# The adjacency test of a graph network moved from the loading to a second read beside layer 1, with the rows' transposes put between the chunks of the first product

## The chip, the cores and the metric

The kernel runs on one core of a Trainium2 chip. The metric is device time in microseconds (us) of one execution. Engines are named as in the profile: PE is TensorE, PEld its weight loads, DVE is VectorE, ACT is ScalarE, POOL is GpSimd, and SPq is the DMA queue issued from SyncE. A load has *landed* when its data is there; the *granted clock* is the share of full speed that the profile records for PE. The batches are worked on in four *pairs*, the nodes in four *blocks* of 512.

## The reference, cut to what matters

```python
# x: 8 x 2048 x 64, adj: 2048 x 2048 fp32; a row of adj has one value where it is not zero
h = relu(layernorm(x)); x = x + L0(h, adj)   # Chebyshev terms h, A h, 2 A(A h) - h, node-wise weights
h = relu(layernorm(x)); x = x + L1(h, adj)   # 3 steps: v = W2 relu(W1 [v, A v] + b1) + b2
h = relu(layernorm(x)); x = x + L2(h, adj)   # one A h, then small matrices
h = relu(layernorm(x)); x = x + L3(h, adj)   # attention with mask adj > 0.5: for this adj a mean over nodes
```

The kernel keeps the adjacency as a 0/1 pattern `BT` (the sign of `adj`, transposed) and the row values apart (`crow`). That holds only if all non-zero values of a row are equal and none exceeds 0.5. So it *tests* the adjacency; if the test fails a general path runs. The test must read every element of `adj` and know its row's maximum.

## The kernel before: the parts that matter

Loading (32 half-rows of 128 x 1024, three buffers) with the test beside it:

```python
def load_adj(nb):                                   # one of 4 node blocks
    for t in range(4):
        i = 4 * nb + t
        for hf in range(2):
            st = prop.tile([P, N // 2], F32, name="st", bufs=3)
            nc.sync.dma_start(st, adj[i*P:(i+1)*P, hf*(N//2):(hf+1)*(N//2)])
            for q in range(2):                      # 8 transposes on PE, sign on ACT
                pt = transposed(...)
                nc.scalar.activation(BT[:, nb, m0:m0+4, t*P:(t+1)*P], pt, AF.Sign)
            c = cols2[:, i, hf:hf + 1]
            nc.vector.tensor_reduce(c, st, axis=AX.X, op=ALU.max)
            nc.vector.scalar_tensor_tensor(         # the test
                junk, st, c, st, op0=ALU.not_equal, op1=ALU.logical_and,
                accum_out=bad2[:, i, hf:hf + 1])
    ...                                             # crow of this block
```

The product that all layers use, 32 matmuls (a high part H and a low part L of the features, 16 chunks), and layer 1, whose step feeds the next one:

```python
def product(hl, nb, name, out, crow, mid=None):
    for m in range(NCH):
        for i in range(2):
            nc.tensor.matmul(ps, hl[m // 4][i][:, m % 4, :], BT[:, nb, m, :], ...)
        if m == NCH // 2 and mid is not None:
            mid()
    nc.vector.tensor_tensor(out, ps, crow, op=ALU.mult)

for s in range(3):                                  # layer 1, one pair of batches
    for nb in range(NB):
        ph = ...                                    # one matmul
        e = product(hl, nb, ..., mid=mid if nb == 3 else None)
        nc.vector.tensor_tensor(e, ph, e, op=ALU.add)
        nc.scalar.activation(g, e, AF.Relu, bias=...)
        if nb in (1, 2): finish(nb - 1)             # bn on PE, then H and L of the next step
    ...
```

The order in the source is not the order on the engines: the scheduler of the framework places each instruction where its data and engine allow.

Of the kernel before, what the change touches and what calls it, by code (L numbers as in the profile page):

```python
# [40 lines left out]
def uniform_path(  # L41
# [53 lines left out]
    def bank(tag, name):  # L95
        return psum.tile([P, 512], F32, tag=tag, name=name)
# [12 lines left out]
    def part(nb):  # L109
        return slice(4 * nb, 4 * nb + 4)  # L110

    def load_x(layer, p, nb):
        acc = block("acc", f"acc_{layer}_{p}_{nb}", 2)
        fill_x(acc, layer, p, nb)
        return acc

    def fill_x(acc, layer, p, nb):
        if layer == 0:
            for bb in range(2):
                nc.sync.dma_start(  # L120
                    acc[:, :, bb * C:(bb + 1) * C],
                    x[2 * p + bb].rearrange("(j p) c -> p j c", p=P)[:, part(nb), :],
                )
        else:
            nc.sync.dma_start(acc, xs[p][:, part(nb), :])
# [41 lines left out]
        nc.vector.tensor_tensor(Lq, src, Hq.bitcast(F32), op=ALU.subtract)  # L167
        return Hq, Lq

    def product(hl, nb, name, out, crow, mid=None):  # L170

        ps = bank("mm", f"bv_{name}")
        for m in range(NCH):
            for i in range(2):
                nc.tensor.matmul(  # L175
                    ps, hl[m // 4][i][:, m % 4, :], BT[:, nb, m, :],
                    start=(m == 0 and i == 0), stop=(m == NCH - 1 and i == 1),
                )
            if m == NCH // 2 and mid is not None:
                mid()  # L180
        nc.vector.tensor_tensor(out, ps, crow, op=ALU.mult)  # L181
        return out

# [17 lines left out]
    def term(k, name):  # L201
        return l0f.tile([P, 512], F32, tag=f"t{k}", name=name, bufs=(4, 4, 2)[k])

    def norm_0(p, nb):
        return norm_relu(load_x(0, p, nb), f"0_{p}_{nb}")


    cols2 = consts.tile([P, NCH, 2], F32, name="cols2")
    bad2 = consts.tile([P, NCH, 2], F32, name="bad2")
    cols = consts.tile([P, NCH, 1], F32, name="cols")  # L210
    pro = ExitStack()
    prop = pro.enter_context(tc.tile_pool(name="prop", bufs=1))

    def load_adj(nb):
        for t in range(4):
            i = 4 * nb + t
            for hf in range(2):
                st = prop.tile([P, N // 2], F32, name="st", bufs=3)
                nc.sync.dma_start(st, adj[i * P:(i + 1) * P, hf * (N // 2):(hf + 1) * (N // 2)])
                for q in range(2):  # L220
                    pt = transposed(
                        lambda m: st[:, (4 * q + m) * P:(4 * q + m + 1) * P], f"adj_{i}_{hf}_{q}"
                    )
                    m0 = 8 * hf + 4 * q
                    nc.scalar.activation(BT[:, nb, m0:m0 + 4, t * P:(t + 1) * P], pt, AF.Sign)  # L225
                c = cols2[:, i, hf:hf + 1]
                nc.vector.tensor_reduce(c, st, axis=AX.X, op=ALU.max)  # L227
                junk = prop.tile([P, N // 2], U8, name="junk")
                nc.vector.scalar_tensor_tensor(  # L229
                    junk, st, c, st, op0=ALU.not_equal, op1=ALU.logical_and,  # L230
                    accum_out=bad2[:, i, hf:hf + 1],
                )
        nc.vector.tensor_tensor(
            cols[:, part(nb), :], cols2[:, part(nb), 0:1], cols2[:, part(nb), 1:2], op=ALU.max
        )
        pg = transposed(lambda t: cols[:, 4 * nb + t, :].to_broadcast([P, P]), f"c_{nb}")
        crow = work.tile([P, 512], F32, tag="crow", name=f"crow_{nb}", bufs=2)
        nc.scalar.copy(crow, pg.rearrange("p t n -> p (t n)"))
        nc.gpsimd.dma_start(crowD[:, nb * 512:(nb + 1) * 512], crow[0:1, :])
        return crow  # L240

    def test():


        w = small.tile([P, NCH, 2], F32, name="w", bufs=1)
        nc.vector.tensor_tensor(w, cols2, cols.to_broadcast([P, NCH, 2]), op=ALU.not_equal)
        nc.vector.tensor_tensor(w, w, cols2, op=ALU.logical_and)
        nc.vector.tensor_tensor(bad2, bad2, w, op=ALU.add)
        for op, lim in ((ALU.is_gt, THRESHOLD), (ALU.is_lt, 0.0)):
            nc.vector.tensor_scalar(w, cols2, lim, None, op0=op)  # L250
            nc.vector.tensor_tensor(bad2, bad2, w, op=ALU.add)
        tot = small.tile([P, 1], F32, name="tot")
        nc.vector.tensor_reduce(tot, bad2.rearrange("p j h -> p (j h)"), axis=AX.X, op=ALU.add)
        pf = bank("tr", "pf")
        nc.tensor.matmul(pf[:1, :1], tot, ones[:, :1], start=True, stop=True)
        nc.vector.tensor_scalar(flag, pf[:1, :1], 0.0, None, op0=ALU.is_gt)




    def term1(p, hl, crow_of):
        t1T, hl1 = [], []

        def back(nb):
            pt = transposed(lambda t: t1T[nb][:, t * P:(t + 1) * P], f"t1_{p}_{nb}")
            hl1.append(halves(pt, f"t1_{p}_{nb}"))

        for nb in range(NB):
            crow = crow_of(nb)
            nm = f"0_{p}_{nb}a"  # L270
            t1T.append(product(
                hl, nb, nm, term(1, f"t1T_{nm}"), crow, mid=(lambda: back(2)) if nb == 3 else None
            ))
            if nb in (1, 2):
                back(nb - 1)
        back(3)
        return t1T, hl1

    t0T, hl = [], []
    for nb in range(NB):  # L280
        z = norm_0(0, nb)
        hl.append(halves(z, f"0_0_{nb}"))
        t0T.append(to_feat(z, term(0, f"t0T_0_{nb}"), f"0_0_{nb}"))
    t1T, hl1 = term1(0, hl, load_adj)
    test()
    pro.close()

    l0p = l0.enter_context(tc.tile_pool(name="l0p", bufs=1))
# [64 lines left out]
    for p in range(NP):  # L353
        if p > 0:
            t1T, hl1 = term1(p, hl, lambda nb: load_crow(nb, f"0_{p}_{nb}a"))
        hl_next, t0T_next = [], []

        def prepare(q):
            if p + 1 < NP:
                h = load_h(p + 1, q, f"0_{p + 1}_{q}")  # L360
                hl_next.append(halves(h, f"0_{p + 1}_{q}"))
                return h

        def prepare_feat(h, q):
            if p + 1 < NP:
                t0T_next.append(to_feat(h, term(0, f"t0T_{p + 1}_{q}"), f"0_{p + 1}_{q}"))

        for nb in range(NB):
            nm = f"0_{p}_{nb}b"
            crow = load_crow(nb, nm)  # L370
            pre = []
            t2T = product(
                hl1, nb, nm, term(2, f"t2T_{nm}"), crow,
                mid=(lambda: pre.append(prepare(2))) if nb == 3 else None,
            )
            if p + 1 < NP:

                for q in ((0, 1), (2, 3), (), ())[nb]:
                    nc.gpsimd.dma_start(hs[p + 1][:, part(q), :], norm_0(p + 1, q))
            if nb == 3:  # L380
                prepare_feat(pre[0], 2)
                h3 = prepare(3)
            node_weights(p, nb, (t0T[nb], t1T[nb], t2T))
            if nb in (1, 2):
                prepare_feat(prepare(nb - 1), nb - 1)
        if p + 1 < NP:
            prepare_feat(h3, 3)
        hl, t0T = hl_next, t0T_next
# [96 lines left out]
        hl.append(halves(h, nm))  # L485




    def layer1(n, p):  # L490
        hl, gT = ops[n]
        steps = 3
        for s in range(steps):
# [22 lines left out]
            for nb in range(NB):  # L516
                nm = f"1_{p}_{s}_{nb}"
                crow = load_crow(nb, nm)
                ph = bank("tr", f"ph_{nm}")
                nc.tensor.matmul(ph, w1v2 if s else w1vT, gT[nb], start=True, stop=True)  # L520
                e = product(hl, nb, nm, feat(f"e_{nm}"), crow, mid=mid if nb == 3 else None)
                nc.vector.tensor_tensor(e, ph, e, op=ALU.add)  # L522
                g = feat(f"g_{nm}")
                nc.scalar.activation(g, e, AF.Relu, bias=b1s if s else b1c)  # L524
                g_new.append(g)
                if nb in (1, 2):
                    finish(nb - 1)
                    if last:
                        prepare(n + 1, nb - 1)
            if last:  # L530
                finish(2)
                prepare(n + 1, 3)
# [5 lines left out]
    def layer2(n, p):  # L538
# [18 lines left out]
        for nb in range(NB):  # L557
            nm = f"2_{p}_{nb}"
            crow = load_crow(nb, nm)
            e = product(  # L560
                hl, nb, nm, feat(f"e_{nm}"), crow,
                mid=(lambda: prepare(n + 1, 2)) if nb == 3 else None,
            )
            finish(nb, e)
            if nb in (1, 2):
                prepare(n + 1, nb - 1)
# [17 lines left out]
        prepare(0, q)  # L584
    for n, (layer, p) in enumerate(items):
        (layer1, layer2)[layer - 1](n, p)


@with_exitstack
# [590 lines left out]
```

## Time and profile before

| | before |
|---|---|
| median of the runs at hand | 1509.42 us (1506.44 to 1510.51) |
| span of the profiled run | 1499.4 us (it took 1501.24, a quick one) |
| first product starts, last of the first four is scaled | 51.3 us, 127.7 us |
| first matmul of the node weights, `y` | 149.7 us |
| layer 1 of the first pair: first product scaled | 840.4 us |
| its three steps, product 0 to product 0 | 36.8, 36.8, 43.0 us |

The slices, the tile `st` and the queue's waits are in the prediction; they show a prologue of 128 us in which DVE is at 6 to 8 tenths, and the test among what holds the three buffers. To read the landmarks: the DVE row `t1T_3a<-bv_3a,crow` is the scaling of the last of the first four products, so its start is the end of the prologue. Before and after:

```profile
127.68 0.69 DVE L181 TENSOR_TENSOR t1T_3a<-bv_3a,crow 128x512 f32<-128x512 f32 x1 [1.67 <-PE bv_3a L175]
```

```profile
103.45 0.69 DVE L181 TENSOR_TENSOR t1T_3a<-bv_3a,crow 128x512 f32<-128x512 f32 x1 [1.89 <-PE bv_3a L175]
```

### The profile page before, as it was taken

What the parts mean: (1) busy time and instruction counts of PE and PEld (TensorE: products, weight loads), DVE (VectorE), ACT (ScalarE), POOL (GpSimd) and SP (SyncE); (2) the same over time, 40 slices, a digit from 0 to 9 for tenths busy, and PEclk for the clock granted to TensorE, in tenths of its full rate; (3) what the DMA queues carried; (4) which work ended last, traced back from release to release, by engine and by line L of the source; (5) the groups of instructions that cost most, each with busy time, mean ns of one, the idle gap of its engine ahead of it and who ended that gap; (6) DMA issues with size and microseconds to landing.
All of it is one profiled execution on the core that took longest, in us unless ns stands there. A gap on an engine that the chain in (4) does not pass through costs nothing.

```text
span 1499.4 us, 15921 instructions
## 1 busy us (share of the span) xinstructions
PE 1312.4 (88%) x6000; PEld 904.8 (60%) x6000; DVE 867.3 (58%) x1879; ACT 188.4 (13%) x317; POOL 242.8 (16%) x234
## 2 busy tenths in 40 slices
PE   2679978997989979899994999999999999898883
PEld 1567434563446534475442877777778777776762
DVE  6885777747777578736785223433523533655453
ACT  3341000000000000000000211211211211111000
POOL 2101111102102021110101001301300300424442
PEclk9999989998999989999997999999999999999897
DMA  3554112112112021110101002301301310323221
GB/s 106 192 189 110 46 53 64 43 46 70 46 36 69 20 70 46 40 53 21 46 29 45 34 28 59 103 29 57 112 28 43 119 32 32 135 70 113 92 85 30
DMA packets 83080, 99.04 MB, mean 66 GB/s; under 512 B 49332, under 2 KB 51380, under 8 KB 82996
## 3 DMA queue, kind: packets, MB, share of 16 engines
q1 hardware_dynamic: 75060, 73.30, 16.6%
q0 software_dynamic: 7936, 24.66, 4.6%
q8 instruction: 49, 0.80, 0.2%
q14 instruction: 35, 0.29, 0.1%
HBM read 73.28 MB, written 24.65 MB: 65 GB/s over the span
## 4 chain that ended last, share of the span: by engine, by line
PE 51%; DVE 24%; issue 12%; POOL 6%; DMA 4%; ACT 1%; SPq 1%; DVEq 0%; POOLq 0%; ACTq 0%
PE bv L175 24%; DVE acc L347 15%; POOL rstd L156 4%; PE y L340 4%; PE bn L466 3%; PE ph L520 3%; PE bv_0a L175 2%; PE bv_0b L175 2%; PE bv_3a L175 2%; PE bv_1a L175 2%; PE bv_2a L175 2%; DMA st<-in_adj_dram 2%; DVE z L157 2%; PE pS L552 1%; DVE var L153 1%
## 5 line engine op out<-in xcount | busy, mean ns | idle before, releaser
L175 PE MATMUL bv<-BT,H 128*128 128x512 f32 x1024 | 424.2, 414 | 0.0
L175 PE MATMUL bv<-BT,L 128*128 128x512 f32 x1024 | 408.3, 399 | 0.9 <-DVE L L167 0.9
L347 DVE SCALAR_TENSOR_TENSOR acc<-y,emb,acc 128x128 f32<-128x128 f32 x1024 | 355.3, 350 | 63.8 <-PE y L340 21.5
L175 PEld LDWEIGHTS bv<-BT,L 128*128 128x128 f32 x1024 | 194.2, 190 | 52.0 <-issue 9.3
L175 PEld LDWEIGHTS bv<-BT,H 128*128 128x128 f32 x1024 | 194.1, 190 | 49.9 <-issue 9.3
L340 PE MATMUL y<-wt,t0T 64*128 64x512 f32 x512 | 149.9, 653 | 67.8 <-DVE acc L347 64.6
L181 DVE TENSOR_TENSOR e<-bv,crow 128x512 f32<-128x512 f32 x64 | 44.2, 691 | 191.6 <-PE bv L175 191.3
L321 POOL DMA_DIRECT2D xs<-acc x32 | 17.8, 556 | 844.0 <-DVE acc L503 352.3
L156 POOL TENSOR_TENSOR rstd<-var,mhalf 128x8 f32<-128x8 f32 x64 | 108.1, 1689 | 220.7 <-DVE var L154 210.3
L340 PEld LDWEIGHTS y<-wt,t0T 64*128 64x128 f32 x512 | 45.3, 192 | 156.4 <-PE y L340 94.1
L151 ACT ACTIVATE sq<-z 128x512 f32<-128x512 f32 x64 | 40.5, 633 | 678.1 <-DVE z L147 668.2
L157 DVE SCALAR_TENSOR_TENSOR z<-z,rstd 128x512 f32<-128x512 f32 x64 | 53.8, 841 | 108.4 <-POOL rstd L156 108.4
L153 DVE TENSOR_REDUCE var<-sq 128x8 f32<-128x512 f32 x64 | 43.8, 685 | 31.2 <-ACT sq L151 31.1
L188 PE MATMUL pt_adj<-ident,st 128*128 128x128 f32 x256 | 40.5, 308 | 22.0 <-DMA st<-in_adj_dram 16.6
L188 PEld LDWEIGHTS pt_adj<-ident,st 128*128 128x128 f32 x256 | 31.9, 157 | 30.3 <-ACT BT L225 23.0
L552 PE MATMUL pS<-z,ones 128*128 128x128 f32 x128 | 22.8, 333 | 29.0 <-DVE z L157 29.0
L507 DVE TENSOR_TENSOR bn<-bn,r1e 128x512 f32<-128x512 f32 x32 | 22.2, 695 | 43.4 <-PE bn L466 43.4
L145 DVE TENSOR_REDUCE mean<-acc 128x8 f32<-128x512 f32 x64 | 43.3, 684 | 4.6 <-DMA acc<-in_x_dram 3.1
L524 ACT ACTIVATE g<-e,b1s 128x512 f32<-128x512 f32 x32 | 23.2, 726 | 178.6 <-DVE e L522 178.6
L147 DVE TENSOR_TENSOR z<-acc,mean 128x512 f32<-128x512 f32 x64 | 43.9, 694 | 1.7
L227 DVE TENSOR_REDUCE cols<-st 128x1 f32<-128x1024 f32 x32 | 38.9, 1218 | 9.8 <-DMA st<-in_adj_dram 9.7
L229 DVE SCALAR_TENSOR_TENSOR junk<-st,cols 128x1024 uint8<-128x1024 f32 x32 | 41.0, 1280 | 0.5
(185 smaller groups left out, 1777.2 us busy)
## 6 DMA issues: line engine op xcount, KB each, us to landing
st<-in_adj_dram SPq DMA_DIRECT2D x32, 512.0 KB, 4.1
crow<-crowD SPq DMA_DIRECT2D x64, 256.0 KB, 3.3
hs<-z POOLq DMA_DIRECT2D x44, 256.0 KB, 2.7
hb<-hs SPq DMA_DIRECT2D x44, 256.0 KB, 4.1
acc<-in_x_dram SPq DMA_DIRECT2D x64, 128.0 KB, 2.8
xs<-acc POOLq DMA_DIRECT2D x32, 256.0 KB, 2.7
acc<-xs SPq DMA_DIRECT2D x32, 256.0 KB, 4.0
out_dram<-acc POOLq DMA_DIRECT2D x32, 128.0 KB, 4.2
```

What stands on the lines that cost most here:

```text
L145: nc.vector.tensor_reduce(mean, groups(xt), axis=AX.X, op=ALU.add)
L147: nc.vector.tensor_tensor(g, groups(xt), mean[:, :, None].to_broadcast([P, 8, C]), op=ALU.subtract)
L153: nc.vector.tensor_reduce(var, groups(sq), axis=AX.X, op=ALU.add)
L156: nc.gpsimd.tensor_tensor(rstd, var, mhalf, op=ALU.pow)
L157: nc.vector.scalar_tensor_tensor(g, g, 0.0, rstd[:, :, None].to_broadcast([P, 8, C]), op0=ALU.max, op1=ALU.mult)
L175: nc.tensor.matmul(ps, hl[m // 4][i][:, m % 4, :], BT[:, nb, m, :], start=(m == 0 and i == 0), stop=(m == NCH - 1 and i == 1),)
L181: nc.vector.tensor_tensor(out, ps, crow, op=ALU.mult)
L188: nc.tensor.transpose(pt[:, t, :], src(t), ident)
L340: nc.tensor.matmul(y[:, bb, :], terms[k][hs_, ts], wt[hs_, k, dg * 512:(dg + 1) * 512], start=(k == 0), stop=(k == K - 1),)
L347: nc.vector.scalar_tensor_tensor(xj, y[:, :, d * C:(d + 1) * C], emb[:, 4 * nb + t, e:e + 1], xj, op0=ALU.mult, op1=ALU.add,)
L466: nc.tensor.matmul(ps[:, t, :], fT[:, t * P:(t + 1) * P], wmat, start=True, stop=True)
L520: nc.tensor.matmul(ph, w1v2 if s else w1vT, gT[nb], start=True, stop=True)
```

## The change

It means to take the test out of the loading, where DVE is full (6 to 8 tenths), and to do it where DVE idles (2 to 5 tenths in layers 1 and 2), on a second read of the adjacency beside layer 1. The loading is taken apart so that the transposes of the next block stand between the chunks of the current product.

```diff
-def load_adj(nb):
-    for t in range(4):
+def load_adj(nb, t):
...
-            nc.vector.scalar_tensor_tensor(junk, st, c, st, op0=ALU.not_equal, op1=ALU.logical_and, ...)
...
 t0T, hl = [], []
 for nb in range(NB):
+    load_adj(0, nb)
     z = norm_0(0, nb)                      # x of the first pair now loaded from the ACT queue
...
-t1T, hl1 = term1(0, hl, load_adj)
-test()
+def rows_between(nb):
+    return {4 * t + 1: (lambda t=t: load_adj(nb + 1, t)) for t in range(4)}   # empty for the last
+t1T, hl1 = term1(0, hl, make_crow, rows_between)
...
+def test(i):
+    for q in range(NB):
+        st = lastp.tile([P, 512], F32, name="st", bufs=2)
+        nc.sync.dma_start(st, adj[i*P:(i+1)*P, q*512:(q+1)*512])
+        nc.vector.scalar_tensor_tensor(junk, st, cols[:, i, :], st, ..., accum_out=bad[:, i, q:q+1])
...
 # layer 1, after each block
+if s < 2 and nb in (0, 2):
+    test(4 * p + 2 * s + nb // 2)          # meant: 16 row groups over four pairs
```

More of the change, by code (lines that the diff above doesn't have):

```diff
@@ L110, in part, with load_x, fill_x @@
         return slice(4 * nb, 4 * nb + 4)
-    def load_x(layer, p, nb):
+    def load_x(layer, p, nb, queue=nc.sync):
         acc = block("acc", f"acc_{layer}_{p}_{nb}", 2)
-        fill_x(acc, layer, p, nb)
+        fill_x(acc, layer, p, nb, queue)
         return acc
-    def fill_x(acc, layer, p, nb):
+    def fill_x(acc, layer, p, nb, queue=nc.sync):
         if layer == 0:
             for bb in range(2):
-                nc.sync.dma_start(
+                queue.dma_start(
                     acc[:, :, bb * C:(bb + 1) * C],
@@ L168, in halves, with product @@
         return Hq, Lq
-    def product(hl, nb, name, out, crow, mid=None):
+    def product(hl, nb, name, out, crow, fill={}):
         ps = bank("mm", f"bv_{name}")
@@ L178, in product @@
                 )
-            if m == NCH // 2 and mid is not None:
-                mid()
+            if m in fill:
+                fill[m]()
         nc.vector.tensor_tensor(out, ps, crow, op=ALU.mult)
@@ L204, in norm_0 @@
     def norm_0(p, nb):
-        return norm_relu(load_x(0, p, nb), f"0_{p}_{nb}")
+        return norm_relu(load_x(0, p, nb, nc.scalar if p == 0 else nc.sync), f"0_{p}_{nb}")
     cols2 = consts.tile([P, NCH, 2], F32, name="cols2")
-    bad2 = consts.tile([P, NCH, 2], F32, name="bad2")
     cols = consts.tile([P, NCH, 1], F32, name="cols")
@@ L212, in uniform_path, with make_crow @@
     prop = pro.enter_context(tc.tile_pool(name="prop", bufs=1))
-    def load_adj(nb):
-        for t in range(4):
-            i = 4 * nb + t
-            for hf in range(2):
-                st = prop.tile([P, N // 2], F32, name="st", bufs=3)
-                nc.sync.dma_start(st, adj[i * P:(i + 1) * P, hf * (N // 2):(hf + 1) * (N // 2)])
-                for q in range(2):
-                    pt = transposed(
-                        lambda m: st[:, (4 * q + m) * P:(4 * q + m + 1) * P], f"adj_{i}_{hf}_{q}"
-                    )
-                    m0 = 8 * hf + 4 * q
-                    nc.scalar.activation(BT[:, nb, m0:m0 + 4, t * P:(t + 1) * P], pt, AF.Sign)
-                c = cols2[:, i, hf:hf + 1]
-                nc.vector.tensor_reduce(c, st, axis=AX.X, op=ALU.max)
-                junk = prop.tile([P, N // 2], U8, name="junk")
-                nc.vector.scalar_tensor_tensor(
-                    junk, st, c, st, op0=ALU.not_equal, op1=ALU.logical_and,
-                    accum_out=bad2[:, i, hf:hf + 1],
-                )
+    def load_adj(nb, t):
+        i = 4 * nb + t
+        for hf in range(2):
+            st = prop.tile([P, N // 2], F32, name="st", bufs=3)
+            nc.sync.dma_start(st, adj[i * P:(i + 1) * P, hf * (N // 2):(hf + 1) * (N // 2)])
+            for q in range(2):
+                pt = transposed(
+                    lambda m: st[:, (4 * q + m) * P:(4 * q + m + 1) * P], f"adj_{i}_{hf}_{q}"
+                )
+                m0 = 8 * hf + 4 * q
+                nc.scalar.activation(BT[:, nb, m0:m0 + 4, t * P:(t + 1) * P], pt, AF.Sign)
+            nc.vector.tensor_reduce(cols2[:, i, hf:hf + 1], st, axis=AX.X, op=ALU.max)
+    def make_crow(nb):
         nc.vector.tensor_tensor(
@@ L240, in load_adj, with term1 @@
         return crow
-    def test():
-        w = small.tile([P, NCH, 2], F32, name="w", bufs=1)
-        nc.vector.tensor_tensor(w, cols2, cols.to_broadcast([P, NCH, 2]), op=ALU.not_equal)
-        nc.vector.tensor_tensor(w, w, cols2, op=ALU.logical_and)
-        nc.vector.tensor_tensor(bad2, bad2, w, op=ALU.add)
-        for op, lim in ((ALU.is_gt, THRESHOLD), (ALU.is_lt, 0.0)):
-            nc.vector.tensor_scalar(w, cols2, lim, None, op0=op)
-            nc.vector.tensor_tensor(bad2, bad2, w, op=ALU.add)
-        tot = small.tile([P, 1], F32, name="tot")
-        nc.vector.tensor_reduce(tot, bad2.rearrange("p j h -> p (j h)"), axis=AX.X, op=ALU.add)
-        pf = bank("tr", "pf")
-        nc.tensor.matmul(pf[:1, :1], tot, ones[:, :1], start=True, stop=True)
-        nc.vector.tensor_scalar(flag, pf[:1, :1], 0.0, None, op0=ALU.is_gt)
-    def term1(p, hl, crow_of):
+    def term1(p, hl, crow_of, between=lambda nb: {}):
         t1T, hl1 = [], []
@@ L271, in term1 @@
             t1T.append(product(
-                hl, nb, nm, term(1, f"t1T_{nm}"), crow, mid=(lambda: back(2)) if nb == 3 else None
+                hl, nb, nm, term(1, f"t1T_{nm}"), crow, fill={**({8: lambda: back(2)} if nb == 3 else {}), **between(nb)}
             ))
@@ L283, in uniform_path @@
         t0T.append(to_feat(z, term(0, f"t0T_0_{nb}"), f"0_0_{nb}"))
-    t1T, hl1 = term1(0, hl, load_adj)
-    test()
+    def rows_between(nb):
+        if nb + 1 == NB:
+            return {}
+        return {4 * t + 1: (lambda t=t: load_adj(nb + 1, t)) for t in range(4)}
+    t1T, hl1 = term1(0, hl, make_crow, rows_between)
     pro.close()
@@ L373, in uniform_path @@
                 hl1, nb, nm, term(2, f"t2T_{nm}"), crow,
-                mid=(lambda: pre.append(prepare(2))) if nb == 3 else None,
+                fill={8: lambda: pre.append(prepare(2))} if nb == 3 else {},
             )
@@ L485, in prepare, with test_end @@
         hl.append(halves(h, nm))
+    bad = lastp.tile([P, NCH, NB], F32, name="bad")
+    def test(i):
+        for q in range(NB):
+            st = lastp.tile([P, 512], F32, name="st", bufs=2)
+            nc.sync.dma_start(st, adj[i * P:(i + 1) * P, q * 512:(q + 1) * 512])
+            junk = lastp.tile([P, 512], U8, name="junk")
+            nc.vector.scalar_tensor_tensor(
+                junk, st, cols[:, i, :], st, op0=ALU.not_equal, op1=ALU.logical_and,
+                accum_out=bad[:, i, q:q + 1],
+            )
+    def test_end():
+        for op, lim in ((ALU.is_gt, THRESHOLD), (ALU.is_lt, 0.0)):
+            w = lastp.tile([P, NCH, 1], F32, name="w", bufs=2)
+            nc.vector.tensor_scalar(w, cols, lim, None, op0=op)
+            nc.vector.tensor_tensor(bad[:, :, 0:1], bad[:, :, 0:1], w, op=ALU.add)
+        tot = lastp.tile([P, 1], F32, name="tot")
+        nc.vector.tensor_reduce(tot, bad.rearrange("p i q -> p (i q)"), axis=AX.X, op=ALU.add)
+        pf = bank("tr", "pf")
+        nc.tensor.matmul(pf[:1, :1], tot, ones[:, :1], start=True, stop=True)
+        nc.vector.tensor_scalar(flag, pf[:1, :1], 0.0, None, op0=ALU.is_gt)
     def layer1(n, p):
@@ L520, in layer1 @@
                 nc.tensor.matmul(ph, w1v2 if s else w1vT, gT[nb], start=True, stop=True)
-                e = product(hl, nb, nm, feat(f"e_{nm}"), crow, mid=mid if nb == 3 else None)
+                e = product(hl, nb, nm, feat(f"e_{nm}"), crow, fill={8: mid} if nb == 3 else {})
                 nc.vector.tensor_tensor(e, ph, e, op=ALU.add)
@@ L561, in layer2 @@
                 hl, nb, nm, feat(f"e_{nm}"), crow,
-                mid=(lambda: prepare(n + 1, 2)) if nb == 3 else None,
+                fill={8: lambda: prepare(n + 1, 2)} if nb == 3 else {},
             )
@@ L586, in uniform_path @@
         (layer1, layer2)[layer - 1](n, p)
+        if n == NP - 1:
+            test_end()
 @with_exitstack
```

## The prediction

The 0.69 us of a 128x512 test is the mean of the 128x512 scaling in the trace before.

> **What bounds the kernel now.** I read four views: the slices of the page, to find stages in which TensorE (PE) is not full; the instructions on the adjacency tile `st` and the waits of the DMA queue, to see what holds the first stage; the timeline of PE there, for single intervals; and the timelines of layer 1, where the moved work goes.
>
> ```profile
> PE   2679978997989979899994999999999999898883
> DVE  6885777747777578736785223433523533655453
> DMA  3554112112112021110101002301301310323221
> ...
> L188 PE MATMUL pt_adj<-ident,st x256: 270/273/476, 31.5 to 121.6; 128*128 128x128 f32 x128
> L227 DVE TENSOR_REDUCE cols<-st x32: 1208/1220/1221, 8.2 to 120.5; 128x1 f32<-128x1024 f32 x32
> L229 DVE SCALAR_TENSOR_TENSOR junk<-st,cols x32: 1273/1280/1286, 9.9 to 121.7; 128x1024 uint8<-128x1024 f32 x32
> L229 DVE DVE_READ_ACCUMULATOR junk<-st,cols x32: 81/84/89, 11.1 to 122.9; 128x1 f32 x32
> ...
> DMA to landing us min/median/max: 3.1/4.1/5.3
> ...
> SPq L219 <- DVE junk L229: 56.9, 24, 3.9
> SPq L219 <- PE pt_adj L188: 25.0, 9, 11.4
> ```
>
> A slice is 37.5 us. In the first three PE is at 2, 6 and 7 tenths, VectorE (DVE) at 6, 8 and 8: this is the prologue, to about 128 us, in which 32 half-rows of the adjacency are loaded, transposed, reduced to their maximum and tested. The last two lines tell who holds the loads: with three `st` buffers a new load waits for the *test* 56.9 us in total and for the transposes 25.0 us, of which one wait is 11.4 us, because PE's first transpose of `st` is at 31.5 us, behind the normalisation of x. So the bound here is a ring of three buffers whose turn is landing (4.1 us) plus transposes plus maximum plus test, served by a DVE that is nearly full. PE's own work to 127.6 us is only about 63 us: four products of 32 x 0.2326 us (the spacing of their matmuls in the timeline) = 30, 256 transposes at 0.109 = 28, other transposes 5.
>
> From the second node block on the limits are others: layer 0 alternates PE and DVE (1024 multiply-adds of 350 ns), layers 1 and 2 have PE at 9 tenths and DVE at 2 to 5. Layer 1 of the first pair, on DVE and then PE:
>
> ```profile
> 867.99 0.69 DVE L181 TENSOR_TENSOR e<-bv,crow 128x512 f32<-128x512 f32 x1 [1.16 <-PE bv L175]
> 868.72 0.69 DVE L522 TENSOR_TENSOR e<-ph,e 128x512 f32<-128x512 f32 x1
> ...
> 867.79 1.02 PE L520 MATMUL ph<-g,w1v 128*128 128x512 f32 x2
> 870.26 1.12 PE L466 MATMUL bn<-w1e,g 128*128 128x128 f32 x8
> ```
>
> At the end of a step the last block's product is scaled at 867.99, added at 868.72, passed through ReLU to 870.16, and PE takes it at 870.26, seven matmuls into the next step. There is no slack: what delays this scaling delays PE.
>
> [...] the trace has 691 ns as the mean of the 128x512 scaling. I use it for the test at 512 columns, which the kernel before has only at 1024. [...] eight transposes took 1.94 us after 3.85 us of idle at 46.70[...].
>
> **The change, part by part.**
>
> *Taken from the prologue.* 32 tests: 32 x (1.20 us spacing + 0.08 read of the accumulator) = 41 us of DVE, and the closing test, 8 small operations of 0.2 us with one matmul, 1.6 us. DVE's 102 us of work before 130 us becomes about 60, so it stops being a limit, and the ring's turn loses the test.
>
> *Reordered.* The first adjacency rows are loaded before x, and the built program's PE order puts each later 128 rows' transposes between the chunks of the product before. First four row groups: a chain remains, since the same ACT queue copies transposes out and issues the second half of x. From the first load at about 1 us I followed normalisation (10 to 14 us for the first block, as now), x's third block issued near 19 us, its result near 31, the fourth near 36; the first product starts then, near 37 us, against 51.3 now. After that 24 half-rows remain. Per half-row PE needs 0.87 us of transposes and four chunks' share, 0.93, plus short waits for ACT: three products 22.3 + 24 x 0.87 + about 8 for waits and other transposes = 51 us. The loads need 24 x 512 KB = 12.6 MB; the best 10 us stretch now moved 244 GB/s, which is 51.6 us. Two limits this close disturb each other: I add 5 us. Product 2 ends near 93, product 3 (7.44 us and two transposes) near 101.5. It now ends at 127.6. Gain: 26 us.
>
> *Start of the node weights.* In the new order 12 instead of all 32 matmuls of the second b-product stand ahead of the first `y`. Now `y` starts at 149.66 although its inputs are ready at about 145.4. 20 x 0.2326 = 4.6 us; the 20 matmuls fall later where PE idles (4 us busy of 10 at 190). Gain: 4.6 us.
>
> *Added in layer 1.* 16.8 MB read again as 64 loads of 256 KB on the SP queue, and 64 tests of 128x512: 0.69 + 0.08 = 0.77 us each, 49 us of DVE, where DVE idles most of the time. The work fits; its order is the question. The scheduler put all 64 into the *first* pair's layer 1, about five per product, and DVE works in order, so a test whose load has not landed holds what stands behind it. Two buffers: a turn is landing plus test plus about 0.1 us. Landing of 256 KB in layer 1 now is 2.5 us for the x blocks and 3.1 for the scaling row. Turn 3.4 to 4.0 us, so 1.7 to 2.0 us per test, and five per product 8.6 to 9.9 us against 9.2 us (four products in 36.8 us). At 1.7 the tests keep pace, and the steps lose some 3 us. At 2.0 I followed the chain: 16 tests before the first step's end hold the scaling at 867.99 back by 6.5 us, PE waits 5.8 us; the second step adds 4.3; the third a few: 14 us. I take the middle: 8 us lost. Two first test loads before the last layer-1 block's load: 1 us more.
>
> Sum: -26 - 4.6 + 8 + 1 = -21.6 us, from 1509 to about 1487.
>
> **The rivals.** *The work is hidden and the loads stream:* if the landing is 2.5 us, layer 1 loses about 3 us, and if the prologue streams at 290 GB/s (short slices of it show that) product 3 ends near 96: -26 - 5.5 - 4.6 + 4 = -32 us, 1477. For it: DVE's idle share in layer 1, and DMA's share below 2 tenths there. Against: the 8 us of waits I counted on PE. *The order of layer 1 becomes the bound:* landing above 3.1 us because two loads, the scaling row and h share the queue; 64 tests x 2.2 = 141 us for a stretch of about 110; loss 25 to 30 us, the gain nearly eaten, 1500 to 1505. For it: the zero slack above, and h's landing median of 4.1. Against: those are landings in busy stretches. *The prologue gains little:* the normalisation chain, [...]puts the first product at 45 rather than 37, and the ring of three stays the limit at 2.4 us a half-row: product 3 ends near 112, gain 15; 1498.
>
> **Range and chances.** Prologue 26 +- 7, start of `y` 4.6 +- 2, layer 1 -9 +- 8; in quadrature about 11 us, 8 in 10 within 1.3 times that: 1472 to 1503. Two per cent is 30.2 us, 1479.2: within reach of the first rival only. Faster by over 2%: 0.27; within 2%: 0.71; slower by over 2%: 0.02, since both losses would have to exceed what I sized and no gain come.
>
> **What would show it.** The DMA queue's wait for `junk` gone before 100 us; first product near 37 us and last of the four ending near 101; `y` three to four us after its first b-product; all 64 tests on DVE in about 105 to 125 us of the first pair's layer 1; DVE waits named as waiting for the test's load, and PE waits at `bn` at the first two step ends of some us, none in the other pairs. The prediction is wrong if the prologue ends outside 94 to 110, if PE in that layer 1 stays full (more gain), or if its steps grow from 36.8 to over 42 us (less).

## The result, and the profile after

Ratios below are the mean time of one kernel's fast runs over that of the other's of the same rounds, so they are not quite the ratio of the medians quoted.

| | before | after |
|---|---|---|
| median (4 runs each) | 1507.93 us | 1486.86 us (1484.68 to 1486.99) |
| ratio, 95% interval | | 0.9859 (0.9834 to 0.9885) |
| first product starts | 51.3 | 38.6 |
| last of the first four scaled | 127.7 | 103.5 |
| first `y` | 149.7 | 120.5 |
| layer 1 begins (first scaling) | 840.4 | 812.4 |
| steps of the first pair | 36.8, 36.8, 43.0 | 43.0, 41.1, 49.9 |
| span of the profiled run | 1499.4 | 1485.2 |

The total is the predicted 1487 almost to the digit. The parts are not: 29 us are won by the first `y`, and some 17 are given back in 134 us of layer 1. The slices of the page after (busy tenths, 37 us each) show both ends:

```profile
PE   3899698997989798999976898999999999888883
DVE  6647787477774777648874566533423523655453
DMA  5870211211112111101014555311301301323320
```

The second and third slices of PE have risen to 8 and 9. Near two thirds, where layer 1 begins, DVE rises to 5 and 6, DMA to 4 and 5 for four slices, and PE falls to 8 twice. The tile `st` and the queue's waits (engine and line, what it waited for, us in total, times, longest):

```profile
L481 DVE SCALAR_TENSOR_TENSOR junk<-st,cols x64: 739/752/754, 797.8 to 933.8; 128x512 uint8<-128x512 f32 x64
...
SPq L217 <- DVE cols L224: 30.1, 23, 3.8
SPq L217 <- PE pt_adj L188: 28.2, 18, 5.1
...
DVE junk L481 <- DMA st<-in_adj_dram: 45.8, 40, 2.6
```

The test is gone from the loading (L217 waits for the maximum and the transposes only). All 64 tests ran from 797.8 to 934.6 us, in the first pair, 2.1 us each. DVE stood 45.8 us before loads of tests that had not landed. What stands behind it at the end of the first step, on DVE:

```profile
840.21 0.75 DVE L481 SCALAR_TENSOR_TENSOR junk<-st,cols 128x512 uint8<-128x512 f32 x1 [1.55 <-DMA st<-in_adj_dram]
840.89 0.69 DVE L518 TENSOR_TENSOR bn<-bn,r1e 128x512 f32<-128x512 f32 x1
841.77 0.75 DVE L481 SCALAR_TENSOR_TENSOR junk<-st,cols 128x512 uint8<-128x512 f32 x1 [0.19 <-DMA st<-in_adj_dram]
...
843.93 0.75 DVE L481 SCALAR_TENSOR_TENSOR junk<-st,cols 128x512 uint8<-128x512 f32 x1 [0.79 <-DMA st<-in_adj_dram]
844.61 0.69 DVE L181 TENSOR_TENSOR e<-bv,crow 128x512 f32<-128x512 f32 x1
```

and the same moment on PE:

```profile
842.89 0.39 PE L175 MATMUL bv<-BT,H 128*128 128x512 f32 x1
846.83 1.16 PE L451 MATMUL bn<-w1e,g 128*128 128x128 f32 x8 [3.55 <-ACT g L535]
...
848.48 0.63 PE L175 MATMUL bv<-BT,L 128*128 128x512 f32 x1
848.90 0.63 PE L175 MATMUL bv<-BT,H 128*128 128x512 f32 x1
```

The last product's matmuls were all issued by 840.41, its scaling waits until 844.61 behind tests, and PE idles 3.55 us. Then comes a second loss: the matmuls after the gap start 0.42 us apart where they start 0.23 apart elsewhere, until about 851.5; the granted clock from 848.06 to 851.48 is 0.50.

A third thing happens in the third step, on the queue of the loads. The next pair's `h` is loaded on SPq too, and there it stands behind a test's load:

```profile
906.95 0.33 SPq L134 DMA_DIRECT2D crow<-crowD  x1
909.41 0.33 SPq L479 DMA_DIRECT2D st<-in_adj_dram  x1
909.83 0.46 SPq L129 DMA_DIRECT2D hb<-hs  x1
```

```profile
915.45 0.66 PE L188 MATMUL pt<-ident,hb 128*128 128x128 f32 x4 [3.27 <-ACT hb L467]
```

The test's load goes out when the test before it (908.63 to 909.38 on DVE) gives its buffer free, and `h` 2.9 us after the scaling row; without tests (experiment 1) it is 0.4 us. PE waits for `h` twice in this layer, 5.0 us in all.

### The profile page after: what moved, and what is told of

Same layout as the page of the kernel before. It is cut to its first block, busy times and chain, and to the rows that moved or that the text cites. A ratio compares the mean times of both kernels' runs of the same rounds, so it can differ in the third digit from the quotient of the medians.

```text
span 1485.2 us, 16148 instructions
## 1 busy us (share of the span) xinstructions
PE 1303.0 (88%) x6000; PEld 902.3 (61%) x6000; DVE 873.0 (59%) x1940; ACT 187.2 (13%) x317; POOL 241.6 (16%) x234
## 4 chain that ended last, share of the span: by engine, by line
PE 38%; DVE 24%; issue 14%; DMA 8%; POOL 5%; ACT 1%; SPq 1%; DVEq 0%; POOLq 0%; ACTq 0%
PE bv L175 19%; DVE acc L332 15%; DMA st<-in_adj_dram 5%; POOL rstd L156 4%; PE y L325 3%; PE bn L451 3%; PE ph L531 2%; DMA hb<-hs 2%; DVE z L157 2%; PE bv_2a L175 1%; PE bv_3a L175 1%; PE bv_0b L175 1%; PE bv_1a L175 1%; PE bv_0a L175 1%; DVE junk L481 1%
## 5 line engine op out<-in xcount | busy, mean ns | idle before, releaser
L175 PEld LDWEIGHTS bv<-BT,H 128*128 128x128 f32 x1024 | 195.0, 191 | 49.9 <-issue 9.3
L481 DVE SCALAR_TENSOR_TENSOR junk<-st,cols 128x512 uint8<-128x512 f32 x64 | 48.0, 750 | 46.0 <-DMA st<-in_adj_dram 45.8
L153 DVE TENSOR_REDUCE var<-sq 128x8 f32<-128x512 f32 x64 | 43.8, 684 | 28.3 <-ACT sq L151 28.3
L565 PEld LDWEIGHTS pS<-z,ones 128*128 128x128 f32 x128 | 17.8, 215 | 38.9 <-DVE z L157 38.9
```

What stands on the lines that cost most here:

```text
L153: nc.vector.tensor_reduce(var, groups(sq), axis=AX.X, op=ALU.add)
L481: nc.vector.scalar_tensor_tensor(junk, st, cols[:, i, :], st, op0=ALU.not_equal, op1=ALU.logical_and, accum_out=bad[:, i, q:q + 1],)
```

## The experiments

Twelve kernels ran. Where two calls are compared, the ratio to the kernel before of the same call is used.

**1. No tests at all, new order** (flags set to zero; the output is right for this input only because its adjacency passes).

```diff
-                if s < 2 and nb in (0, 2):
-                    test(4 * p + 2 * s + nb // 2)
+    nc.vector.memset(bad, 0.0)
```

> The changed kernel with its 64 tests and the second read left out (flags set to zero, closing sum kept). Theory 1, the second read costs by holding VectorE's queue behind loads that have not landed: all of what the first pair's layer 1 lost comes back, 17 us by the profile's landmarks, so about 1470 us, and the first pair's steps are back at 36.8 us. Theory 2, the size of the prediction, 9 us: about 1478. Theory 3, the second read is hidden and the lost time in that layer 1 is run-to-run spread: 1487, as the changed kernel. Prologue as in the changed kernel: last of the four first products near 103.5 us.

Measured: 1465.23 us, ratio 0.9746 (0.9715 to 0.9777); steps of the first pair 36.6, 36.6, 42.4. The difference of the ratios, 0.9859 less 0.9746, is 17 us of 1505 (the medians, from two calls, differ by 21.6). So theory 1 holds in its size: the second read costs about 17 us, about twice what was predicted. The two traces say where. The windows from the first scaling of layer 1 to that of the second pair, columns us, PE, PEld, DVE, ACT, POOL busy, granted clock, DMA share, GB/s, first after, then this kernel:

```profile
812.37:946.35 133.98, 121.77 (x555) 95.74 (x554) 82.70 (x185) 20.08 (x33) 12.88 (x13) 0.96 0.51 161
```

```profile
811.58:927.13 115.55, 115.55 (x553) 92.11 (x552) 43.26 (x70) 19.71 (x32) 12.91 (x13) 1.00 0.17 58
```

Of the 18.4 us, 12.2 are idle PE (133.98 less 121.77) and 6.2 are PE work that took longer (121.77 against 115.55 for the same instructions but two), at a granted clock of 0.96 instead of 1.00. The idle time is five gaps: 0.92, 3.55 and 2.74 us before `bn`, which needs a scaling that tests held up (the last two at the ends of the first two steps), and 3.27 and 1.73 us before the transposes of `h`. From about 1 us after the end of the gaps of 3.55, 2.74 and 3.27 us the granted clock was 0.50 to 0.52 for 3.2 to 3.4 us (848.06 to 851.48, 888.90 to 892.30, 916.40 to 919.60), and after the first two of these 128x512 matmuls started 0.42 to 0.43 us apart; after the gaps of 0.92 and 1.73 us it was 1.00 (836.43 to 840, 929 to 937). (The gaps are counted from the profile's ends of matmuls, which are modelled; the gap of 2.74 us is 3.14 from start to start.) So the second read held up the SPq queue as well as DVE.

**2 and 3. The two halves of the prologue's change apart.** The kernel before with only the test left out; and the new order with the test kept in the loading and no second read.

```diff
 # 2: kernel before
-                nc.vector.scalar_tensor_tensor(junk, st, c, st, ..., accum_out=bad2[:, i, hf:hf + 1])
 # 3: kernel after
+            nc.vector.scalar_tensor_tensor(junk, st, c, st, ..., accum_out=bad2[:, i, hf:hf + 1])
-                if s < 2 and nb in (0, 2):
-                    test(4 * p + 2 * s + nb // 2)
```

> The kernel before with the adjacency test left out of the loading (flags set to zero), its order kept. Theory 1, the test's VectorE time and its place in the turn of the three buffers is what held the prologue: the first product still starts near 51 us, but the last of the four ends near 110 instead of 127.6, and the time falls by 15 to 18 us, to about 1491. Theory 2, the order (adjacency behind x, transposes in blocks) held it: at most 5 us come, 1503 or more.

> The changed kernel's order of the prologue, but the test kept beside the loading (32 tests 1024 wide), no second read. Theory 1 (test in the ring is what held): VectorE has its 41 us again, the last of the four first products ends near 118 and the time is about 1498. Theory 2 (the order is the gain): first product near 40 us and the last near 106, time about 1475. With the two others this makes a two by two table: if the gains of order and of removal add, their sum is that of the kernel without tests, 38 us against before; if each alone gives little and both together much, they are two limits in a row.

Measured: 1499.88 us, ratio 0.9961 (0.9939 to 0.9983), and 1487.38 us, ratio 0.9874 (0.9847 to 0.9901). The ends of the prologue, one line each from the DVE timelines of experiment 2, of 3 and of 1:

```profile
126.72 0.69 DVE L181 TENSOR_TENSOR t1T_3a<-bv_3a,crow 128x512 f32<-128x512 f32 x1 [1.95 <-PE bv_3a L175]
```

```profile
120.03 0.69 DVE L181 TENSOR_TENSOR t1T_3a<-bv_3a,crow 128x512 f32<-128x512 f32 x1 [1.90 <-PE bv_3a L175]
```

```profile
103.76 0.69 DVE L181 TENSOR_TENSOR t1T_3a<-bv_3a,crow 128x512 f32<-128x512 f32 x1 [1.91 <-PE bv_3a L175]
```

| last of the first four scaled at | test in the loading | test out |
|---|---|---|
| old order | 127.7 | 126.7 |
| new order | 120.0 | 103.8 |

Alone, the removal is worth 1 us at this landmark and the order 8; together 24. At the first `y` it is 4, 7 and 29 us (149.7; 145.7, 142.4, 120.8), and in the whole time the removal alone is worth 6 us by its ratio. The theories that gave the gain to one half alone (an end at 110 for the removal, at 106 for the order) both fall; those that had little come of it alone were near (5 us by the medians in experiment 2; an end near 118 in experiment 3, though its time lies between both theories), and the last clause of the expectation of experiment 3 is what came. They are two limits in a row. One expectation missed besides: in experiment 2 the first product started at 44.3 us and not near 51. (The ratio of experiment 3 also holds the effect of experiments 8 to 10; these ends of the prologue hardly do. They repeat within 1.3 us in the two profiles of the kernel before, but stand at 131.8 in experiments 9 and 10, where only an unused tile was added: 1 us is within that spread, 24 are not.) The new order has three parts, the rows first, x from the ACT queue and the transposes between the chunks; no run takes these apart. The queue's waits show the exchange, for experiment 2 and then 3:

```profile
SPq L220 <- PE pt_adj L188: 39.9, 16, 9.3
```

```profile
SPq L218 <- DVE junk L228: 56.1, 24, 6.9
```

With the test out and the old order, the wait for the test turns into waits for the transposes (25.0 us before, 39.9 here) and for the maximum (30.3). With the test in and the new order, the test holds the loads as before, 56.1 us against 56.9. Note also what experiment 3 says of the change: with the test left in the loading the new order makes 1487.38 us, the whole change 1486.86. So, within the noise, taking the test out to a second read bought nothing as it was placed.

**4. The kernel before again,** for a second profile.

> The kernel before once more, for a second profile. The first profile fell on a fast run of 1501 us where the median is 1508. If that run was fast in one stage, the landmarks here differ from it in that stage: the last of the four first products near 127.6, first y near 149.7, layer 1's first product near 840, each within 2 us if the difference is spread; time near 1508.

Measured: 1503.43 us (one run, state unknown), first `y` at 150.9 and layer 1 at 843.2 where the first profile had 149.7 and 840.4. The landmarks of one kernel differ by 1 to 3 us between runs, spread over the stages. So the 14 us between the two first profiles and the 21 us between the medians are no contradiction.

**5. The same tests, spread and tied to their pair.** Each pair of tests reads its row maxima through a copy that also needs a result `g` of its own step, so that the scheduler can't place it earlier.

```diff
-    def test(i):
-        for q in range(NB):
+    def test(i, qs, pin):
+        c = lastp.tile([P, 1], F32, name="ct", bufs=2)
+        nc.vector.scalar_tensor_tensor(c, pin[:, 0:1], 0.0, cols[:, i, :], op0=ALU.mult, op1=ALU.add)
+        for q in qs:
...
-                if s < 2 and nb in (0, 2):
-                    test(4 * p + 2 * s + nb // 2)
+                if nb < 3 and 3 * s + nb < 8:
+                    j = 3 * s + nb
+                    test(4 * p + j // 2, (2 * (j % 2), 2 * (j % 2) + 1), g)
```

> The changed kernel with the same 64 tests and the same second read, but each pair of tests made to wait, through its copy of the row maxima, for a ReLU result of its own step: two tests a product, first two or three products of a step only, 16 tests in each of the four pairs. Theory 1 (a test costs only when VectorE stands behind a load that has not landed): each load has a whole product of 9 us to land, so VectorE's waits for the tests' loads fall from 46 us to under 5, the first pair's steps are back at 36.6 to 37 us, time 1466 to 1469. Theory 2 (the tests' VectorE work or the 16.8 MB themselves cost): 64 tests still delay, 1478 or more.

Measured: 1468.37 us, ratio 0.9767 (0.9737 to 0.9797); steps of the first pair 36.4, 36.6, 42.8, and in the list of DVE's waits none names the tests' loads. The timeline of one product:

```profile
832.19 0.16 DVE L478 SCALAR_TENSOR_TENSOR ct<-g,cols 128x1 f32<-128x1 f32 x1 [0.18 <-ACT g L539]
832.38 0.75 DVE L485 SCALAR_TENSOR_TENSOR junk<-st,ct 128x512 uint8<-128x512 f32 x1
...
833.66 0.74 DVE L485 SCALAR_TENSOR_TENSOR junk<-st,ct 128x512 uint8<-128x512 f32 x1
```

The two tests run without a wait, because their loads had the whole product before to land. The bytes and the DVE work are the same as in the change; theory 1 holds, and theory 2 falls. By the ratios 14 of the 17 us come back (0.9859 less 0.9767); the first pair's layer 1 takes 115.8 us, against 134.0 in the change and 115.6 without tests.

**6. The same groups of four, only tied to their pair and step.** As 5, but with the places that the change wrote.

```diff
-                    test(4 * p + 2 * s + nb // 2)
+                    test(4 * p + 2 * s + nb // 2, range(NB), g)
```

> The changed kernel with each test made to wait for a result of its own pair and step, in the groups of four that the change wrote (after blocks 0 and 2 of the first two steps). Tells whether the spread inside a product is needed or only the pair: theory 1 (with two buffers the first two tests of a group find their data landed, the other two wait some 2 us each, inside a product of 9 us): at most 3 us lost, 1468 to 1471. Theory 2 (a group of four holds the end of a step, block 3's scaling): 4 pairs times 2 steps of 1 to 2 us, 1476 to 1482.

Measured: 1469.96 us, ratio 0.9738 (0.9709 to 0.9766), theory 1. DVE still waited for loads of tests,

```profile
DVE junk L485 <- DMA st<-in_adj_dram: 33.5, 23, 2.4
```

33.5 us against 45.8 in the change, and the first pair's steps are 36.6, 36.6 and 42.4 as without tests. These waits cost the steps nothing: they lie inside a product, with nothing on the path due behind them for some us. So the change as it was *meant* was good; the scheduler's bringing all 64 tests forward into one pair is what cost.

**7. Four buffers for the tests' loads instead of two,** tests still where the scheduler puts them.

```diff
-        st = lastp.tile([P, 512], F32, name="st", bufs=2)
+        st = lastp.tile([P, 512], F32, name="st", bufs=4)
```

> The changed kernel with four buffers of 256 KB for the tests' loads in place of two; the scheduler still puts all 64 tests into the first pair, now in seven to eight products. Theory 1 (the turn of two buffers, landing plus test, sets the pace of 2.1 us a test): about half of VectorE's waits go and the loss in the first pair falls from 18 to at most 8 us, 1473 or so. Theory 2 (the two loads already share one queue's bandwidth, so deeper rings only lengthen each landing): no change, 1486. Theory 3 (VectorE's own work is next: 53 us of tests and some 21 of its own in about 69 us of products): a loss of 5 to 12 us stays, 1470 to 1478, with VectorE at 9 tenths or more in the first two steps.

Measured: 1476.66 us, ratio 0.9810 (0.9793 to 0.9827); 0.9810 less 0.9746 is some 10 us still lost; steps 43.4, 35.5, 42.4. The waits for the tests' loads fell from 45.8 to 15.5 us and the pace from 2.1 to 1.2 us a test. The windows of the first 68 us of layer 1, after and here:

```profile
812.00:880.00 68.00, 63.53 (x285) 49.92 (x284) 40.70 (x94) 8.31 (x13) 0.00 (x0) 0.97 0.51 158
```

```profile
812.00:880.00 68.00, 62.17 (x273) 48.70 (x272) 54.69 (x135) 8.24 (x13) 0.00 (x0) 0.95 0.70 223
```

DVE rises from 40.70 to 54.69 us, 8 tenths: the work is denser, and the longest single wait of PE at `bn` is 4.7 us against 3.6. Theory 2 falls (the loads do go faster, 223 GB/s against 158); theories 1 and 3 both hold in part (DVE did not reach the 9 tenths that theory 3 named): the deeper ring takes away waits, and more tests run ahead of a step's end. Ahead of the last scaling of the first step DVE ran 24 tests in the change and 40 here, and that scaling came at 848.2 us instead of 844.6.

**8 to 10. A thing that no one had changed on purpose.** The second step of the second pair takes 36.45 us after and 36.78 before, and it is the matmuls: in a product they start 0.2324 us apart before (mean of 596 spacings from 950 to 1150 us) and 0.2298 after. The change removes three small tiles, and by the address lists of the built programs that moves H and L from, for one block, 166784 to 166464, and `BT` from 17920 to 17792. Experiment 8 puts both back with unused tiles in the kernel of experiment 1; 9 and 10 move them in the kernel before.

```diff
+    pad1 = consts.tile([P, 32], F32, name="pad1")            # 8: BT, H and L as before (128 + 192 bytes)
+    pad2 = small.tile([P, 48], F32, name="pad2", bufs=1)
...
+    pad2 = small.tile([P, 16], F32, name="pad2", bufs=1)     # 9: H and L by 64 bytes, BT stays
...
+    pad1 = consts.tile([P, 16], F32, name="pad1")            # 10: BT, H and L all by 64 bytes
```

> The changed kernel without tests (1465.2 us), with two unused tiles of 128 and 192 bytes that put the adjacency tile and the H and L tiles back at the addresses they have in the kernel before; nothing else moves on PE but these addresses. In four kernels the spacing of matmuls in a product was 0.2324 or 0.2325 us where these addresses were those of before, and 0.2298 to 0.2303 where they were not. Theory 1 (addresses set the spacing): spacing 0.2325 here and a time of 1470 to 1473. Theory 2 (something else of the new order): 0.2300 and 1465.

> The kernel before with one unused tile of 64 bytes that moves H and L by 64 bytes (H of one block from 166784 to 166848) and leaves the adjacency tile at 17920. Theory 1a (what matters is where H and L lie: multiples of 128 bytes slow, odd multiples of 64 fast) and theory 1b (what matters is the distance between H and the adjacency tile): spacing 0.2300 and a time 6 to 8 us under before, 1498. Theory 2 (neither; the padded kernel measured something else): 0.2325 and 1505.

> The kernel before with one unused tile of 64 bytes ahead of the adjacency tile, so that it, H and L all move by 64 bytes and their distance stays. Theory 1a (where H and L lie): spacing 0.2300, time 1498. Theory 1b (their distance): spacing 0.2325, time 1505. A third case, the adjacency tile's own place, would show as a spacing that differs from both.

| kernel | `BT`, H of one block | H less `BT`, in units of 128 bytes | spacing, us | ratio |
|---|---|---|---|---|
| before | 17920, 166784 | 1163 | 0.2324 | 1 |
| 8 (no tests, padded) | 17920, 166784 | 1163 | 0.2324 | 0.9790 |
| 1 (no tests) | 17792, 166464 | 1161.5 | 0.2303 | 0.9746 |
| 9 (before, H moved) | 17920, 166848 | 1163.5 | 0.2298 | 0.9920 |
| 10 (before, all moved) | 17984, 166848 | 1163 | 0.2324 | 0.9980 |

The same can be read off two scalings in a row, which one product of 9.1 us parts, in the timelines of experiments 8 and 9:

```profile
979.19 0.69 DVE L181 TENSOR_TENSOR e<-bv,crow 128x512 f32<-128x512 f32 x1 [6.91 <-PE bv L175]
988.37 0.69 DVE L181 TENSOR_TENSOR e<-bv,crow 128x512 f32<-128x512 f32 x1 [5.75 <-PE bv L175]
```

```profile
1003.24 0.69 DVE L181 TENSOR_TENSOR e<-bv,crow 128x512 f32<-128x512 f32 x1 [6.90 <-PE bv L175]
1012.34 0.69 DVE L181 TENSOR_TENSOR e<-bv,crow 128x512 f32<-128x512 f32 x1 [5.67 <-PE bv L175]
```

The differences are 9.18 and 9.10 us; in experiment 10 it is 9.18 (1006.60 to 1015.78). The spacing follows the distance between H and `BT`, not the place of either: theory 1b. It was 1% longer at the one distance tried that is a whole multiple of 128 bytes, and shorter at the two that are an odd multiple of 64. Whether it is that rule or these distances, and why, stays open. What it is worth: 64 products of 31 spacings by 0.0025 us are 5 us in layers 1 and 2, as an estimate from these spacings, and layer 0 has 32 more products. By the ratios it is 0.0044 (7 us, experiment 8 against 1) and 0.0080 (12 us, experiment 9), of which experiment 10 may show 3 to be noise. Experiment 8 took 1475.83 us, 3 more than theory 1 named, and 5 of the 11 us between its profile and that of experiment 1 lie in layer 0 (first `y` to layer 1: 696.2 against 690.8), where the kernel before, at the same addresses, also takes 690.8. So not all of that ratio is the spacing. (Experiments 9 and 10 took 1498.89 and 1506.16 us, as theory 1b named.) What the spacing is worth in the whole time is an estimate, then: 5 to 7 us.

**11 and 12. Better versions,** both on top of experiment 5: x of the first pair loaded first (two more buffers), and four instead of three buffers for the adjacency rows.

```diff
+    for nb in range(NB):                            # 11: before the first load_adj
+        a = block("acc", ...) if nb < 2 else prop.tile([P, 4, 2 * C], F32, ...)
+        fill_x(a, 0, 0, nb, nc.scalar)
...
-            st = prop.tile([P, N // 2], F32, name="st", bufs=3)
+            st = prop.tile([P, N // 2], F32, name="st", bufs=4)     # 12, without 11
```

> The spread tests, and all four blocks of x loaded first (two more buffers), which takes away the 10 us in which PE waited for the third block's normalisation. Theory 1 (the normalisation chain sets the first product's start): first product near 30 us instead of 39, last of the four ending near 94 to 97 instead of 103.5, time 1458 to 1461. Theory 2 (the loads of the adjacency set the end whatever starts first: 16.8 MB at 250 GB/s are 67 us plus a product): last of the four still ends at 100 or later, time 1465 or more.

> The kernel with spread tests, with four buffers instead of three for the adjacency rows in the prologue. Theory 1 (the ring of three is still the limit of the prologue, with 30 us of waits for the maximum and 28 us for the transposes in the queue): these waits fall by half and the last of the four first products ends at 98 or earlier instead of 104, time 1462 or less. Theory 2 (the loads run at the bandwidth that the chip gives, 240 to 290 GB/s in slices of 10 us): no change, 103 to 104, 1468.

Measured: 1464.14 us, ratio 0.9722 (0.9702 to 0.9742), and 1465.81 us, ratio 0.9701 (0.9680 to 0.9721). With x first, the first product starts at 30.4 instead of 38.7 us but the last of four is scaled at 100.6 instead of 104.5: 8 us earlier at the start, 4 at the end, nearer to theory 2. With four buffers it is 99.9, short of the 98 that theory 1 asked for. Its queue, and the window from 40 to 90 us:

```profile
SPq L217 <- PE pt_adj L188: 50.3, 24, 6.2
SPq L217 <- DVE cols L224: 10.9, 10, 2.4
```

```profile
40.00:90.00 50.00, 49.32 (x306) 39.94 (x305) 33.30 (x39) 30.11 (x55) 6.23 (x7) 0.98 0.78 253
```

The waits for the maximum fell from 31.9 to 10.9 us and those for the transposes rose from 28.9 to 50.3: PE is busy 49.3 of 50 us, against 43.8 in experiment 5, at the same 0.8 of the DMA engines' time. PE is nearly full there; that it is now the limit is a reading of this line, and no run tests it. Both versions beat the kernel before (by 2.8 and 3.0%) and the change; which of the two is better is not settled, as they ran on different chips, and they can't simply be joined: the build refuses it, with 20 KB per partition asked for the prologue and 17.4 left.

## Why the prediction was right, and where it was right by luck

The total was 1487.0 against 1486.86. Its terms, against what was measured:

| term | predicted | measured | from |
|---|---|---|---|
| end of the first four products | -26 | -24.2 | profiles before and after |
| start of `y` | -4.6 | -5.0 | from last scaling to `y`: 22.0, now 17.0 |
| layer 1 of the first pair, with the first tests | +9 | +17 to +18 | experiment 1 |
| matmul spacing | none | -5 to -7 (estimate) | experiments 8 to 10 |
| sum | -21.6 | -17 to -19 | medians: -21.1; profiles: -14.2 |

The landmarks of the two profiles add up to their own difference: -24.2 to the last scaling, -5.0 to `y`, +1.1 in layer 0, +17.4 in the first pair's layer 1, -3.5 from the second pair on, -14.2 in all. The profile before fell on a quick run, 7 us under the median, so the medians differ by more.

*The prologue* was right in size and in mechanism, and more so than was shown there: the prediction spoke of the test as what held the ring. Experiments 2 and 3 show that the test's removal alone would have been worth 1 us there (6 in the whole time); it was right because it also followed the reordered chain. It put the first product near 37 (38.6) and the last end near 101.5 (103.5). The 5 us that it added for loads and PE disturbing each other were the author's estimate. From the first product's start to the last scaling it took 64.9 us, where the prediction has 64.5 with them and 59.5 without; PE waited there 4.9 us in all for rows that had not landed, and the queue of the rows waited 28.2 us for PE's transposes in the whole prologue; the loads moved 236 to 289 GB/s in the slices from 40 to 90, with PE busy 7.8 to 9.3 of each 10 us. No run takes these 5 us apart.

*The start of `y`* was right in size and in mechanism: in the trace after, 12 matmuls of the second b-product stand ahead of the first `y`, as it said, and layer 0 behind it took only 1.1 us longer. The traces of experiments 2 and 3 add what the count hangs on: 32 matmuls and 22.0 us before, 19 and 19.0 with the test out in the old order, 32 and 22.4 with the test in in the new. It takes the test's removal; the new order alone did not do it.

*Layer 1* is the step that failed: "I take the middle: 8 us lost"; it lost 17 to 18. The mechanism was the one described, a test whose load has not landed holding a scaling, for 7.2 of the 12.2 us in which PE idled. The prediction had two branches, 1.7 us a test for 3 us lost and 2.0 us a test for 14, and took the mean of the outcomes. The pace was 2.1 us, so it was the second branch (the landing was 3.0 us in the median, at the upper end of what was assumed, and a test took 0.75 + 0.08 us instead of 0.69 + 0.08: the time of the scaling, which the prediction used for it, did not fit). That branch counted PE's waits as 5.8 and 4.3 and a few more; the waits at the first two step ends were smaller, 3.6 and 2.7, with 0.9 more inside the first step. The other 5.0 us are waits for the next pair's `h` behind tests' loads on one queue, which the prediction names only in a rival ("share the queue"). So its total, 14 against 12.2, was near in part by luck. What it left out is PE work that took longer, 6.2 us, at a granted clock of 0.50 after the three longest gaps, though the prediction itself shows such a case (eight transposes in 1.94 us at 46.70, where the granted clock was 0.50; at 39.45, where it was 1.00, eight took 1.06). The clause that would make it wrong, steps over 42 us, did fire: 43.0 us in the first step. Of the signs, the tests took 137 us where 105 to 125 were named; PE's waits at `bn` came at the first two step ends, as named.

*The matmul spacing* was not in the prediction at all. It offset most of the error in layer 1. Without it the change would have come to about 1492 to 1494, by that estimate, still inside the range. That the middle landed on the measured value is therefore luck in two terms; the prologue and the range are not.

*The rivals.* "Hidden, and the loads stream" falls: the loads were in order behind two buffers. "The order of layer 1 becomes the bound" was nearer, with the shared queue that it names, though the turn was 2.1 us a test and not 2.2 and the loss 17 and not 25 to 30. "The prologue gains little" falls with an end at 103.5.

## What to carry to other kernels

Work moved to an idle engine cost little here once its data was there when its turn came (by the ratios some 3 us in experiment 5, against 17 as first placed): an early place in DVE's list with a late load held everything behind it, and so did its place in a queue of loads, so tie moved work to the place where it is meant to run and give its load one stage of lead. Where two limits follow each other, the removal of one alone can show little (1 and 8 us here, 24 together), so try them together before giving either up. And count, behind each wait of PE, the slower matmuls after it (6.2 us beside 12.2 us of waiting here); and when the same loop runs 1% faster after an unrelated edit (0.2298 us a matmul instead of 0.2324 here), look at where its tiles have come to lie.
